# Softmax sums of the second attention layer: two query blocks per pass, straight from the statistics' tile, and the squares weighted once per batch

## The chip, the cores and the metric

The kernel runs on one core of one Trainium2 chip. A core has five engines that run side by side and meet through semaphores: TensorE (PE in the profile; its weight loads are shown apart as PEld), VectorE (DVE), ScalarE (ACT), GpSimd (POOL) and SyncE (SP), and 16 DMA engines that the queues of SP and POOL feed. The metric is the device time of one execution in microseconds (us). A figure given as a median is one of several executions; the profile shows one execution.

## The reference, cut to what matters

The input is 8 images of 512 channels by 1024 positions, all in float32. Two attention layers follow one another. Only the second is touched. With 8 heads of 64 channels it computes

```
attn = einsum('bhdq,bhdT->bhqT', q, k) * scale
attn = einsum('gh,bhqT->bgqT', w_head, attn)          # mixes the heads
attn = softmax(attn, axis=-1)
mean = mean(attn, axis=(-2, -1)); var = var(attn, axis=(-2, -1))
attn = (attn - mean) / sqrt(var + EPS) * in_gamma + in_beta
out  = einsum('bhqT,bhdT->bhqd', attn, v) ... @ w_proj.T + b_proj
```

So each row of the mixed scores needs its sum of exponentials Z (the softmax divides by it), and each head needs the sum over all rows of (sum of squared exponentials) / Z squared, from which the variance follows. The mean is known: a row of a softmax adds up to 1.

## The kernel before, in words

The first layer takes the first 1800 us or so. Then the eight images (batches) go through the second layer one after the other. The 1024 query rows of a batch are cut into 8 blocks of 128, called p = 0 to 7. A block is pipelined over three steps; step p does, in four parts t = 0 to 3, the scores of block p, the head mixing, the exponentials, the transposes and the statistics of block p-1, and the products with V of block p-2. `Attention1.step` writes that order out by hand, and it is the order on every engine: nothing moves past it.

What one block goes through:

- `scores` (L1628): PE makes q times k; ACT copies the result from PSUM to the tile `raw` (L1640).
- `regroup` (L1646): SP issues 16 DMAs of 256 KB per block that rearrange `raw` into the tile `re`, so that heads lie on partitions. `raw` has two buffers, so a copy of the next block waits until the DMAs have read the old contents.
- `mix` (L1665): PE mixes the heads; ACT takes the exponentials into `e` (L1678), two instructions for each of the four parts s of a block. The tile `e` has two buffers.
- `flip` (L1693): DVE transposes `e` into `et`. `moments` (L1704): DVE runs four `bn_stats` over the same `e`. Each leaves, for every partition, count, mean and sum of squared deviations of 256 even and of 256 odd elements; the access pattern is such that these are the two rows r of the part.
- `values` (L1720): PE multiplies V with `et` into an accumulator in PSUM; `leave` (L1736): ACT copies it into the output tile, in the place of q.
- `sums` (L1746 to L1750): three small DVE instructions turn mean and squared deviation into the sum (256 times the mean) and the sum of squares, in the tile `zz`.
- `totals` (L1757): PE adds these over the four partition groups with two matmuls against a 0/1 matrix `sel`; the results lie in PSUM. Below, this place in the order is called **stop p** (stop 0 to 7 of a batch). Stop p lies in part t = 1 of step p + 2, between products with V (L1720) and scores (L1628), which the mixing (L1665) follows.
- `reciprocals` (L1769 to L1789): DVE takes 1/Z, copies Z to `zs`, squares 1/Z, multiplies with the sum of squares and adds to a running sum `s2`: five small instructions, each block. 1/Z goes by one DMA to DRAM (`zd`, 4 KB, L1772) and by a second one back, broadcast over 64 partitions (`rzb`, 256 KB, L1779). POOL issues both, and for the last block SP.
- `divide` (L1811): after two blocks, when both halves of `rzb` are there, POOL multiplies the outputs of the pair by it (DVE for the last pair).
- At the end of a batch `instance` and `instance_end` make the variance from `s2`; `check` looks at the range of Z.

PSUM buffers for scores and mixing are three (`m_psum`), for products with V and the stops two (`acc_psum`). Tiles of the pool `stat` have two buffers if nothing else is said.

Of the kernel before, what the change touches and what calls it, by code (L numbers as in the profile page):

```python
# [18 lines left out]
P = 128  # L19
# [448 lines left out]
def tile_two_attention_layers(  # L468
# [33 lines left out]
    dram = ctx.enter_context(tc.tile_pool(name="dram", bufs=1, space=DRAM))  # L502
# [13 lines left out]
    def const_tile(name, shape, dt=F32):  # L516
        return const.tile(shape, dt, tag=name, name=name)
# [15 lines left out]
    ones = const_tile("ones", [P, P])  # L533
# [30 lines left out]

    sel = const_tile("sel", [P, 32])
    nc.vector.reduce_sum(sel, ident.rearrange("p (c j) -> p j c", c=4), axis=AX.X)
    init.close()


# [3 lines left out]
    chk = const_tile("chk", [P, 2, NCHK])  # L573
# [123 lines left out]
    with ExitStack() as l0:  # L697
# [4 lines left out]
        zpool = l0.enter_context(tc.tile_pool(name="zpool", bufs=2))  # L702
        stat = l0.enter_context(tc.tile_pool(name="stat", bufs=2))
# [563 lines left out]
    with ExitStack() as l1:  # L1267
# [5 lines left out]
        zpool = l1.enter_context(tc.tile_pool(name="zpool1", bufs=1))  # L1273
        stat = l1.enter_context(tc.tile_pool(name="stat1", bufs=2))
# [17 lines left out]
        NF = 5  # L1292
        re_t = repool.tile([P, NF + 4, 2, FB], F32, tag="re", name="re")
# [319 lines left out]
        class Attention1:  # L1613
            def __init__(self, b):
                self.b = b
                self.raw, self.e, self.et, self.acc, self.bn = {}, {}, {}, {}, {}
                self.pieces = []
                self.zs = stat.tile([32, NT, 32], F32, tag="zs", name=f"zs_{b}", bufs=1)
                self.s2 = stat.tile([32, 32], F32, tag="s2", name=f"s2_{b}")

            def scores(self, p, i):

# [74 lines left out]

            def moments(self, p, s):

                if s == 0:  # L1700
                    self.bn[p] = stat.tile([P, 4, 4, 6], F32, tag="bn1", name=f"bn1_{self.b}_{p}")
                e = self.e.pop((p, s))
                for a in range(4):
                    nc.vector.bn_stats(  # L1704
                        self.bn[p][:, s, a], e[:, :, a].rearrange("p r k -> p k r")
                    )

            def values(self, p, u, *parts):
# [29 lines left out]
                        acc[two * D : two * D + D].rearrange("p a (r x) -> p a r x", r=2),  # L1738
                    )

            def sums(self, p):

                bn = self.bn.pop(p).rearrange("p s a (r k) -> p r (s a) k", k=3)
                zz = stat.tile([P, 3, 2, 16], F32, tag="zz", name=f"zz_{self.b}_{p}")
                mean, m2 = bn[..., 1], bn[..., 2]
                nc.vector.tensor_scalar_mul(  # L1746
                    zz[:, 0::2], mean.unsqueeze(1).to_broadcast([P, 2, 2, 16]), float(2 * P)
                )
                nc.vector.tensor_mul(zz[:, 1], mean, zz[:, 0])
                nc.vector.tensor_add(zz[:, 1], zz[:, 1], m2)  # L1750
                self.zz = zz

            def totals(self, p):

                ps = acc_psum(f"z1_{self.b}_{p}")
                for m in range(2):
                    nc.tensor.matmul(  # L1757
                        ps[:D, ts(m, 32)],
                        self.zz[:, m : m + 2].rearrange("p m r c -> p (m r c)"), sel,
                        start=True, stop=True,  # L1760
                    )
                self.reciprocals(p, ps)

            def reciprocals(self, p, ps):

                b = self.b
                z, z2 = ps[:32, 0:32], ps[:32, 32:64]
                rz = stat.tile([32, 32], F32, tag="rz", name=f"rz1_{b}_{p}")
                nc.vector.reciprocal(rz, z)  # L1769
                zd = dram.tile([H, P], F32, tag=f"zd_{b}_{p}", name=f"zd_{b}_{p}")  # L1770
                queue = nc.sync if p == NT - 1 else nc.gpsimd
                queue.dma_start(  # L1772
                    out=zd.rearrange("g (x q) -> x g q", q=4),
                    in_=rz.rearrange("x (g q) -> x g q", q=4),
                )
                if p % 2 == 0:
                    self.rzb = zpool.tile([P, T], F32, tag="rzb", name=f"rzb_{b}_{p}")
                h = p % 2 * D
                queue.dma_start(  # L1779
                    out=self.rzb[h : h + D], in_=zd.rearrange("g i -> (g i)").partition_broadcast(D)  # L1780
                )
                nc.vector.tensor_copy(self.zs[:, p], z)
                r2 = stat.tile([32, 32], F32, tag="r2", name=f"r2_{b}_{p}")
                nc.vector.tensor_mul(r2, rz, rz)  # L1784
                if p == 0:
                    nc.vector.tensor_mul(self.s2, r2, z2)
                else:
                    nc.vector.tensor_mul(r2, r2, z2)
                    nc.vector.tensor_add(self.s2, self.s2, r2)  # L1789

            def check(self):

                b = self.b
                zs = self.zs.rearrange("p t c -> p (t c)")
                junk = zpool.tile([P, T], F32, tag="rzb", name=f"junk_{b}")[:32, : NT * 32]
                cnt = stat.tile([32, 2], F32, tag="cnt", name=f"cnt_{b}")
                nc.vector.tensor_scalar(
                    junk, zs, Z_MAX, 0.0, ALU.is_lt, ALU.add, accum_out=cnt[:, 0:1]
                )
                nc.vector.tensor_scalar(  # L1800
                    junk, zs, 1.0 / RZ_MAX, 0.0, ALU.is_gt, ALU.add, accum_out=cnt[:, 1:2]
                )
                nc.vector.tensor_add(cnt[:, 0:1], cnt[:, 0:1], cnt[:, 1:2])
                nc.vector.tensor_scalar(
                    chk[:32, 1, B * H + b : B * H + b + 1], cnt[:, 0:1],
                    -(2.0 ** 60), 2.0 ** 61 * NT * 32, ALU.mult, ALU.add,
                )

            def divide(self, n, engine=nc.vector):
# [3 lines left out]
            def instance(self):  # L1813

                b = self.b
                self.sb = stat.tile([32, H], F32, tag="isb", name=f"isb_{b}")
                nc.vector.reduce_sum(
                    self.sb, self.s2.rearrange("p (g q) -> p g q", q=4), axis=AX.X
                )

            def instance_end(self, ps=None):
                b = self.b
                if ps is None:
                    ps = small_psum1(f"pi_{b}")
                nc.tensor.matmul(ps[:, :H], ones[:32], self.sb, start=True, stop=True)
# [21 lines left out]
            def step(self, p, t, ag):  # L1847

                new, old, older = p < NT, p >= 1, p >= 2
                if t == 0:  # L1850
# [3 lines left out]
                    if older:  # L1854
                        self.values(p - 2, 0, 2, 3)
                        self.leave(p - 2, 0)
                        self.sums(p - 2)
                        if p % 2 == 0 and p >= 4:
                            self.divide(p // 2 - 2, nc.gpsimd)
                    if old:  # L1860
# [2 lines left out]
                elif t == 1:  # L1863
                    if older:
                        self.values(p - 2, 1, 0)
                        self.flip(p - 1, 0)
                        self.totals(p - 2)
                        self.moments(p - 1, 0)
                    if new:
                        self.scores(p, 3)  # L1870
# [51 lines left out]
        for b in range(B):  # L1922
            more = b + 1 < B
            a = Attention1(b)
# [37 lines left out]
            ag.flush()  # L1962
            k_leave()
            last = NT - 1
            a.sums(last)
            if not more:
                a.values(last, 0, 2, 3)
                a.leave(last, 0)
                a.values(last, 1, 0, 1, 2, 3)
                a.leave(last, 1)  # L1970
                a.totals(last)
                a.instance()
                out1_last(a)
                continue
# [3 lines left out]
            load_wv(b + 1)  # L1978
            a.values(last, 1, 0, 1, 2, 3)
            a.leave(last, 1)  # L1980
            a.totals(last)
            a.instance()
            k_leave()
            k_go(4, 3)
# [84 lines left out]
```

## Time and profile before

| | us |
|---|---|
| runs | 3997.65, 3999.17, 4006.88 (median 3999.17) |
| profiled execution, its own time | 3999.31 |
| span of the profile (first to last instruction) | 3997.5 |
| PE busy (share of the span) | 3885.5 (97%) |
| DVE busy | 2834.6 (71%) |
| ACT busy | 1971.3 (49%) |
| POOL busy | 128.5 (3%) |
| granted TensorE clock, mean | 0.995 |

How to read it: the shares are means over very different stages. In the second layer a batch takes about 277 us; of these some 170 us are the nine steps of the attention, the rest are the projections, where PE works alone. Inside the steps DVE is nearly as full as PE (18 to 25 us of DVE work in a step of 21 to 26 us), so which of the two makes the other wait has to be read from the waits and the timeline, place by place.

### The profile page before, as it was taken

The numbers are of one execution on the slowest core, as the hardware profiler recorded it, in microseconds if no ns is written. First come the engines' busy times: TensorE is split into PE (matmuls) and PEld (weight loads), VectorE is DVE, ScalarE is ACT, GpSimd is POOL, SyncE is SP. The second block draws the span as 40 slices with busy tenths as digits, with TensorE's granted clock in tenths as the row PEclk, the third lists the DMA queues.
The fourth block names the chain that finished last, engine by engine and source line by source line (L and its number), as shares of the span: only waits on it lengthen the run. The fifth ranks groups of instructions, "written<-read, shape, count | busy, mean of one in ns | idle before, by whom it ended". The sixth has DMA issues, their size and how long they took to land.

```text
span 3997.5 us, 95841 instructions
## 1 busy us (share of the span) xinstructions
PE 3885.5 (97%) x41932; PEld 1826.1 (46%) x41932; DVE 2834.6 (71%) x4124; ACT 1971.3 (49%) x2431; POOL 128.5 (3%) x150
## 2 busy tenths in 40 slices
PE   8999999999999999999999999999999999999997
PEld 4353535344343535344544535545545445445354
DVE  4748475766657584857958949859769679588597
ACT  1726363544536271615717528437257166175274
POOL 0000000000000000000100000000001000000010
PEclk9999999999999999999999999999999999999999
DMA  3313131111121111217828749658469288397384
GB/s 121 120 48 117 46 120 48 62 59 66 53 83 54 72 68 61 75 66 184 230 92 226 190 120 237 173 137 227 148 164 228 99 210 207 97 232 198 107 219 127
DMA packets 245883, 519.10 MB, mean 130 GB/s; under 512 B 47312, under 2 KB 54480, under 8 KB 238800
## 3 DMA queue, kind: packets, MB, share of 16 engines
q1 hardware_dynamic: 238912, 497.95, 43.2%
q0 software_dynamic: 6544, 14.94, 1.7%
q8 instruction: 331, 5.42, 0.6%
q14 instruction: 96, 0.79, 0.1%
HBM read 197.16 MB, written 46.92 MB: 61 GB/s over the span
## 4 chain that ended last, share of the span: by engine, by line
PE 81%; DVE 13%; ACT 2%; DMA 2%; issue 2%; SPq 0%; DVEq 0%
PE s L1084 11%; PE a L1110 11%; PE a L1720 7%; PE s L1628 7%; DVE bn L1704 6%; PE pk_p L902 6%; PE pq_p L902 5%; PE pv L1454 5%; PE pv_p L902 5%; DVE et L1693 5%; PE pp_p L902 5%; PE pk L1379 4%; PE pq L1379 4%; PE pp L1379 4%; PE m L1665 4%
## 5 line engine op out<-in xcount | busy, mean ns | idle before, releaser
L1693 DVE STREAM_TRANSPOSE et<-e 128x2048 f32<-128x2048 f32 x256 | 587.3, 2294 | 88.7 <-ACT e L1678 86.8
L1720 PEld LDWEIGHTS a<-et,v 128*64 128x64 f32 x16384 | 509.2, 138 | 296.2 <-issue 247.6
L1704 DVE BATCH_NORM_STATS2 bn<-e 128x6 f32<-128x512 f32 x1024 | 634.3, 675 | 0.0
L1089 ACT ACTIVATE e<-s 128x1024 f32<-128x1024 f32 x512 | 497.2, 1026 | 234.5 <-PE s L1084 232.1
L1640 ACT COPY raw<-s 128x1024 f32<-128x1024 f32 x480 | 470.2, 1018 | 226.1 <-PE s L1628 197.5
L1720 PE MATMUL a<-et,v 128*64 128x64 f32 x16384 | 557.0, 225 | 12.1 <-DVE et L1693 11.4
L1678 ACT ACTIVATE e<-m 128x1024 f32<-128x1024 f32 x512 | 496.2, 1021 | 126.5 <-PE m L1665 54.2
L1097 DVE TENSOR_TENSOR zacc<-zacc,e 128x1024 f32<-128x1024 f32 x384 | 468.7, 1221 | 87.2 <-ACT e L1089 64.9
L1628 PE MATMUL s<-k,q 64*64 64x512 f32 x4096 | 516.0, 608 | 6.2 <-DVE q L1493 3.1
L1084 PE MATMUL s<-q,k 64*64 64x512 f32 x4096 | 490.1, 593 | 2.3 <-ACT e L1089 2.3
L1110 PE MATMUL a<-e,v 64*64 64x512 f32 x4096 | 484.1, 589 | 0.0
L1665 PE MATMUL m<-re,wmix 32*32 32x512 f32 x8192 | 315.3, 604 | 19.3 <-DMA re<-raw 17.8
L1110 PEld LDWEIGHTS a<-e,v 64*64 64x64 f32 x4096 | 156.7, 133 | 282.8 <-issue 282.2
L1084 PEld LDWEIGHTS s<-q,k 64*64 64x64 f32 x4096 | 147.9, 133 | 275.2 <-issue 240.7
L1628 PEld LDWEIGHTS s<-k,q 64*64 64x64 f32 x4096 | 127.7, 132 | 220.8 <-issue 78.2
L1454 PE MATMUL pv<-wv,y 128*128 128x512 f32 x480 | 212.1, 597 | 0.0
L1736 ACT COPY q<-a 64x256 f32<-64x256 f32 x256 | 93.7, 366 | 184.7 <-PE a L1720 182.7
L1772 POOL DMA_DIRECT2D zd<-rz x56 | 34.7, 619 | 3449.0 <-DVE r L1784 3449.0
L1454 PEld LDWEIGHTS pv<-wv,y 128*128 128x128 f32 x480 | 89.3, 190 | 116.9 <-issue 110.3
L1665 PEld LDWEIGHTS m<-re,wmix 32*32 32x32 f32 x8192 | 66.7, 103 | 148.9 <-ACT raw L1640 58.6
L1458 ACT COPY v<-pv 128x512 f32<-128x512 f32 x30 | 17.6, 585 | 218.7 <-PE pv L1454 218.7
L1095 DVE TENSOR_TENSOR zacc<-e,e 128x1024 f32<-128x1024 f32 x64 | 78.3, 1223 | 56.1 <-ACT e L1089 56.1
(315 smaller groups left out, 3942.4 us busy)
## 6 DMA issues: line engine op xcount, KB each, us to landing
re<-raw SPq DMA_DIRECT2D x1024, 256.0 KB
left_q<-left_q SPq DMA_DIRECT2D x17, 1792.0 KB
left_p<-left_p SPq DMA_DIRECT2D x17, 1792.0 KB
left_k<-left_k SPq DMA_DIRECT2D x10, 1792.0 KB
x<-in_x_dram SPq DMA_DIRECT2D x32, 512.0 KB
rzb<-zd SPq DMA_DIRECT2D x128, 128.0 KB
x<-x SPq DMA_DIRECT2D x64, 256.0 KB
y<-x SPq DMA_DIRECT2D x32, 512.0 KB
```

Of the source, the lines that this page charges most:

```text
L902: nc.tensor.matmul(out, st, mv, start=start, stop=(k == 1), skip_group_check=True)
L1084: nc.tensor.matmul(ps[c * D : c * D + D, m], k[r, hp, k0 : k0 + D], q[r, hp, ts(f, FB)], start=True, stop=True,)
L1089: nc.scalar.activation(e[i], ps, AF.Exp, scale=S0 * S0)
L1110: nc.tensor.matmul(acc[g][a][m * D : m * D + D], v[rows, kc, ts(2 * hp + m, D)], e[i][rows, m], start=(kc == 0), stop=(kc == NG - 1),)
L1379: nc.tensor.matmul(self.ps[m][:, i], w[:, left, k * HC + i * P : k * HC + i * P + P], right[:, k], start=(k == 0 and m != 2), stop=(k == 1 ...
L1454: nc.tensor.matmul(ps[:, m], y_t[b][:, c, ts(2 * i + m, P)], w[:, c], start=(c == 0), stop=(c == NCC - 1),)
L1628: nc.tensor.matmul(ps[c * D : c * D + D, m], qo_t[b][r, p, hp, ts(c, D)], k_t[b][r, hp, ts(kh, FB)], start=True, stop=True,)
L1665: nc.tensor.matmul(ps[a // 2][c * 32 : c * 32 + 32, a % 2].rearrange("p (r h k) -> p h r k", r=2, h=2), wmix[rows].rearrange("p g i -> p ( ...
L1678: nc.scalar.activation(e[:, :, 2 * h : 2 * h + 2].rearrange("p r a k -> p a r k"), ps[h].rearrange("p a (r k) -> p a r k", r=2), AF.Exp,)
L1693: nc.vector.transpose(self.et[p, u].rearrange("p kb (r st a) g q -> p st kb r (a g q)", r=2, st=2)[:, st], self.e[p, s].rearrange("p r a ( ...
L1704: nc.vector.bn_stats(self.bn[p][:, s, a], e[:, :, a].rearrange("p r k -> p k r"))
L1720: nc.tensor.matmul(acc[two * D : two * D + D, s].rearrange("p (x q) -> p x q", q=4), v_t[b][:, kb, ts(g, D)], et[:, kb, :, g], start=(kb = ...
```

## The change

`moments` collects the statistics of two blocks, 2n and 2n+1, in one tile. `sums` and `totals` then run once per pair, in the step in which the odd block had them; the even block's stop no longer exists. At the stop that is left three matmuls read the statistics' tile itself: the means against `sel256` (the 0/1 matrix times 256, made once at the start), the squared deviations against `sel`, and the squared means (times 256) against `sel`, added in PSUM. Only the squared means need a DVE instruction (`sq`). DVE then takes 1/Z of 64 rows and copies sum and sum of squares to `zs`. What weighted the squares block by block goes to `instance`, once per batch over all four pairs: reciprocal, square, product and reduction over 128 elements per partition, in a free slot of `re`.

The rows of a pair lie on 64 partitions as (block t, column c, row r), so 1/Z leaves in four DMAs of 2 KB (for r, for t) in place of two of 4 KB, and comes back in two of 256 KB, one right behind the other, where they were one per step. For the last pair SP issues all six.

```diff
+    sel256 = const_tile("sel256", [P, 32])
+    nc.vector.tensor_scalar_mul(sel256, sel, float(2 * P))
...
-                self.zs = stat.tile([32, NT, 32], F32, tag="zs", name=f"zs_{b}", bufs=1)
-                self.s2 = stat.tile([32, 32], F32, tag="s2", name=f"s2_{b}")
+                self.zs = stat.tile([64, NCH, 64], F32, tag="zs", name=f"zs_{b}", bufs=1)
...
+                n = p // 2
+                if s == 0 and p % 2 == 0:
+                    self.bn[n] = stat.tile(
+                        [P, 2, 4, 4, 6], F32, tag="bn1", name=f"bn1_{self.b}_{n}"
+                    )
...
-                zz = stat.tile([P, 3, 2, 16], F32, tag="zz", name=f"zz_{self.b}_{p}")
-                mean, m2 = bn[..., 1], bn[..., 2]
-                nc.vector.tensor_scalar_mul(
-                    zz[:, 0::2], mean.unsqueeze(1).to_broadcast([P, 2, 2, 16]), float(2 * P)
-                )
-                nc.vector.tensor_mul(zz[:, 1], mean, zz[:, 0])
-                nc.vector.tensor_add(zz[:, 1], zz[:, 1], m2)
...
+            def sums(self, n):
+                mean = self.stats(n)[:, :, 1]
+                self.sq = stat.tile([P, 64], F32, tag="sq", name=f"sq_{self.b}_{n}", bufs=1)
+                nc.vector.scalar_tensor_tensor(
+                    self.sq, mean, float(2 * P), mean, ALU.mult, ALU.mult
+                )
...
+            def totals(self, n):
+                b, last = self.b, n == NCH - 1
+                bn = self.stats(n)
+                ps = acc_psum(f"z1_{b}_{n}")
+                nc.tensor.matmul(ps[:64, :32], bn[:, :, 1], sel256, start=True, stop=True)
+                for i, x in enumerate((bn[:, :, 2], self.sq)):
+                    nc.tensor.matmul(ps[:64, 32:64], x, sel, start=(i == 0), stop=(i == 1))
+                rz = stat.tile([64, 32], F32, tag="rz", name=f"rz1_{b}_{n}")
+                nc.vector.reciprocal(rz, ps[:64, :32])
+                nc.vector.tensor_copy(self.zs[:, n], ps[:64, :64])
+                zd = dram.tile([2, H, P], F32, tag=f"zd_{b}_{n}", name=f"zd_{b}_{n}")
+                queue = nc.sync if last else nc.gpsimd
+                for r in range(2):
+                    for t in range(2):
+                        queue.dma_start(
+                            out=zd[t].rearrange("g (r c q) -> r c g q", r=2, q=4)[r],
+                            in_=rz[32 * t + r : 32 * t + 32 : 2].rearrange("c (g q) -> c g q", q=4),
+                        )
+                self.rzb = zpool.tile([P, T], F32, tag="rzb", name=f"rzb_{b}_{n}")
+                for t in range(2):
+                    queue.dma_start(
+                        out=self.rzb[t * D : t * D + D],
+                        in_=zd[t].rearrange("g i -> (g i)").partition_broadcast(D),
+                    )
...
-                r2 = stat.tile([32, 32], F32, tag="r2", name=f"r2_{b}_{p}")
-                nc.vector.tensor_mul(r2, rz, rz)
-                if p == 0:
-                    nc.vector.tensor_mul(self.s2, r2, z2)
-                else:
-                    nc.vector.tensor_mul(r2, r2, z2)
-                    nc.vector.tensor_add(self.s2, self.s2, r2)
...
             def instance(self):
+                scr = re_t[:64, NF + 3, 0]
+                z, z2 = self.zs[:, :, :32], self.zs[:, :, 32:]
...
+                nc.vector.reciprocal(r, z)
+                nc.vector.tensor_mul(r, r, r)
+                nc.vector.tensor_mul(
+                    s2, r.rearrange("p n (g q) -> p n g q", q=4),
+                    z2.rearrange("p n (g q) -> p n g q", q=4),
+                )
                 nc.vector.reduce_sum(
...
-                        self.sums(p - 2)
+                        if p % 2:
+                            self.sums(p // 2 - 1)
...
-                        self.totals(p - 2)
+                        if p % 2:
+                            self.totals(p // 2 - 1)
```

More of the change, by code (lines that the diff above doesn't have):

```diff
@@ L1698, in moments @@
             def moments(self, p, s):
-                if s == 0:
-                    self.bn[p] = stat.tile([P, 4, 4, 6], F32, tag="bn1", name=f"bn1_{self.b}_{p}")
+                n = p // 2
[3 more added lines that the diff above has]
+                    )
                 e = self.e.pop((p, s))
@@ L1704, in moments @@
                     nc.vector.bn_stats(
-                        self.bn[p][:, s, a], e[:, :, a].rearrange("p r k -> p k r")
+                        self.bn[n][:, p % 2, s, a], e[:, :, a].rearrange("p r k -> p k r")
                     )
@@ L1739, in leave @@
                     )
-            def sums(self, p):
-                bn = self.bn.pop(p).rearrange("p s a (r k) -> p r (s a) k", k=3)
-                zz = stat.tile([P, 3, 2, 16], F32, tag="zz", name=f"zz_{self.b}_{p}")
-                mean, m2 = bn[..., 1], bn[..., 2]
-                nc.vector.tensor_scalar_mul(
-                    zz[:, 0::2], mean.unsqueeze(1).to_broadcast([P, 2, 2, 16]), float(2 * P)
-                )
-                nc.vector.tensor_mul(zz[:, 1], mean, zz[:, 0])
-                nc.vector.tensor_add(zz[:, 1], zz[:, 1], m2)
-                self.zz = zz
@@ L1753, in totals @@
[L1753 to L1760, printed above, removed]
-                    )
[L1762 to L1774, printed above, removed]
-                )
[L1776 to L1782, printed above, removed]
-                r2 = stat.tile([32, 32], F32, tag="r2", name=f"r2_{b}_{p}")
-                nc.vector.tensor_mul(r2, rz, rz)
-                if p == 0:
-                    nc.vector.tensor_mul(self.s2, r2, z2)
-                else:
-                    nc.vector.tensor_mul(r2, r2, z2)
-                    nc.vector.tensor_add(self.s2, self.s2, r2)
@@ new lines, in stats @@
+            def stats(self, n):
+                return self.bn[n].rearrange("p t s a (r k) -> p (t s a r) k", k=3)
+            def sums(self, n):
[3 more added lines that the diff above has]
+                    self.sq, mean, float(2 * P), mean, ALU.mult, ALU.mult
+                )
+            def totals(self, n):
+                b, last = self.b, n == NCH - 1
+                bn = self.stats(n)
+                del self.bn[n]
+                ps = acc_psum(f"z1_{b}_{n}")
[18 more added lines that the diff above has]
+                        in_=zd[t].rearrange("g i -> (g i)").partition_broadcast(D),
+                    )
@@ L1791, in check @@
             def check(self):
                 b = self.b
-                zs = self.zs.rearrange("p t c -> p (t c)")
-                junk = zpool.tile([P, T], F32, tag="rzb", name=f"junk_{b}")[:32, : NT * 32]
-                cnt = stat.tile([32, 2], F32, tag="cnt", name=f"cnt_{b}")
+                zs = self.zs[:, :, :32]
+                junk = zpool.tile([P, T], F32, tag="rzb", name=f"junk_{b}")[
+                    :64, : NCH * 32
+                ].rearrange("p (n c) -> p n c", n=NCH)
+                cnt = stat.tile([64, 2], F32, tag="cnt", name=f"cnt_{b}")
@@ L1804, in check @@
                 nc.vector.tensor_scalar(
-                    chk[:32, 1, B * H + b : B * H + b + 1], cnt[:, 0:1],
-                    -(2.0 ** 60), 2.0 ** 61 * NT * 32, ALU.mult, ALU.add,
+                    chk[:64, 1, B * H + b : B * H + b + 1], cnt[:, 0:1],
+                    -(2.0 ** 60), 2.0 ** 61 * NCH * 32, ALU.mult, ALU.add,
                 )
@@ L1815, in instance @@
                 b = self.b
-                self.sb = stat.tile([32, H], F32, tag="isb", name=f"isb_{b}")
+                self.sb = stat.tile([64, H], F32, tag="isb", name=f"isb_{b}")
+                scr = re_t[:64, NF + 3, 0]
+                z, z2 = self.zs[:, :, :32], self.zs[:, :, 32:]
+                r = scr[:, : NCH * 32].rearrange("p (n c) -> p n c", n=NCH)
+                s2 = scr[:, NCH * 32 : 2 * NCH * 32].rearrange("p (g n q) -> p n g q", n=NCH, q=4)
+                nc.vector.reciprocal(r, z)
[4 more added lines that the diff above has]
+                )
                 nc.vector.reduce_sum(
-                    self.sb, self.s2.rearrange("p (g q) -> p g q", q=4), axis=AX.X
+                    self.sb,
+                    scr[:, NCH * 32 : 2 * NCH * 32].rearrange("p (g x) -> p g x", g=H), axis=AX.X,
                 )
@@ L1824, in instance_end @@
                     ps = small_psum1(f"pi_{b}")
-                nc.tensor.matmul(ps[:, :H], ones[:32], self.sb, start=True, stop=True)
+                nc.tensor.matmul(ps[:, :H], ones[:64], self.sb, start=True, stop=True)
                 var = stat.tile([P, H], F32, tag="ivar", name=f"ivar_{b}")
@@ L1964, in tile_two_attention_layers @@
             last = NT - 1
-            a.sums(last)
+            a.sums(NCH - 1)
             if not more:
@@ L1970, in tile_two_attention_layers @@
                 a.leave(last, 1)
-                a.totals(last)
+                a.totals(NCH - 1)
                 a.instance()
@@ L1980, in tile_two_attention_layers @@
             a.leave(last, 1)
-            a.totals(last)
+            a.totals(NCH - 1)
             a.instance()
```

## The prediction

> **What bounds the kernel now.** First the page's busy shares and chain, then who waits on PE, then the timeline around the stops, then the DMA queues.
>
> ```profile
> PE 3885.5 (97%) x41932; PEld 1826.1 (46%) x41932; DVE 2834.6 (71%) x4124; ACT 1971.3 (49%) x2431; POOL 128.5 (3%) x150
> PE 81%; DVE 13%; ACT 2%; DMA 2%; issue 2%; SPq 0%; DVEq 0%
> L1757 PE MATMUL z<-sel,zz 128*64 128x32 f32 x256 | 24.9, 220 | 32.8 <-DVE zz L1750 29.1 <-ACT e L1678 3.6
> ...
> PE z L1757 <- DVE zz L1750: 29.1, 27, 2.1
> PE m L1665 <- DMA re<-raw: 17.8, 11, 3.3
> PE z L1757 <- ACT e L1678: 3.6, 18, 0.4
> PE m L1665 <- ACT e L1678: 1.4, 8, 0.2
> ```
>
> PE is the bound. It idles 112 us in the whole span (3997.5 - 3885.5), and the largest single wait is the one at the stops: 32.8 us before L1757, nearly all of it for `zz`. So DVE time counts only where it ends a wait of PE. The small DVE instructions that go are some 104 us busy (64 blocks by 1.62 us, the means of L1746 to L1789 added up); the new ones come to some 35 us. Were DVE the bound, that would be 68 us; it is not.
>
> Stop 0 and stop 4 of the second batch:
>
> ```profile
> 2131.58 1.94 ACT L1678 ACTIVATE e<-m 128x1024 f32<-128x1024 f32 x2 [0.48 <-ACT q L1736]
> 2133.32 0.21 DVE L1750 TENSOR_TENSOR zz<-zz,bn 128x32 f32<-128x32 f32 x1
> 2133.68 0.39 PE L1757 MATMUL z<-sel,zz 128*64 128x32 f32 x4 [1.22 <-DVE zz L1750]
> 2134.00 1.09 PE L1628 MATMUL s<-k,q 64*64 64x512 f32 x8
> 2135.02 1.16 PE L1665 MATMUL m<-re,wmix 32*32 32x512 f32 x32
> ...
> 2217.13 1.94 ACT L1678 ACTIVATE e<-m 128x1024 f32<-128x1024 f32 x2 [0.64 <-ACT q L1736]
> 2219.70 0.39 PE L1757 MATMUL z<-sel,zz 128*64 128x32 f32 x4 [1.66 <-DVE zz L1750]
> 2220.01 1.09 PE L1628 MATMUL s<-k,q 64*64 64x512 f32 x8
> 2221.03 1.16 PE L1665 MATMUL m<-re,wmix 32*32 32x512 f32 x32
> ```
>
> In brackets stands PE's idle time. A stop itself takes 0.31 us of PE (2219.70 to 2220.01). Over eight batches the idle time before stops 0 to 7 adds up to 9.8, 1.5, 3.4, 1.9, 13.0, 1.4, 1.8 and 0 us. The even stops, which go, hold 28.0 of the 32.8.
>
> **The change, part by part.** *Even stops: what comes next.* Without a stop PE goes on with the scores (1.02 us) and then the mixing, which needs the second exponential's PSUM buffer back (the row "m waits for e": 1.4 us in 8 places). At stop 0 PE would be ready at 2133.68 - 1.22, done with the scores at 2133.48, but the exponentials end at 2131.58 + 1.94 = 2133.52; with 0.06 for the signal the mixing starts at 2133.58 instead of 2135.02: 1.44 us, in each of 8 batches alike, 11.5 us. At stop 4 the same sum gives 2219.13 instead of 2221.03, the idle time plus 0.24: 13.0 + 8 x 0.24 = 14.9 us. At stop 2 (idle about 0.5 us) the exponentials allow 0.72 us in six batches, 0.60 in one and nothing in one: 4.9 us. Stop 6 has no idle time in seven batches; its 0.31 us each make 2.2 us. In the last batch DVE leads after stop 6 (PE later waits 5.33 us for a transpose): the three `zz` that delay a transpose from about 3930.15 to 3930.67 and the 0.87 us of the five small instructions behind it go: 1.4 us. Sum 34.9 us.
>
> *Does DVE follow?* After stop 4 of the second batch PE is 1.9 us earlier. The second transpose (L1693, 2224.99 to 2227.2) moves up by the 0.5 us or more that DVE saved before and the 0.6 us of small instructions behind the first one, to an end near 2226.05; the products that need it move from 2229.20 to 2227.2. It holds, with 1 us spare.
>
> *Odd stops.* Three matmuls in place of two: 0.31 x 6/4 = 0.47 us, 0.16 more, 32 times: 5.1 us lost. The first needs only `bn`, the third `sq`, one instruction (about 0.23 us, as L1746) for three. The 0.2 us of idle time at stops 1, 3 and 5 remains: there ACT's first exponential, not DVE, releases the stop (the row with 18 waits). About 0.9 us of the 4.8 goes. Net 4.2 us lost.
>
> *Strided weights.* The stops load `bn` with 12 bytes between elements. No weight load in the trace is strided. The nearest row, the moving operand of L1720 in runs of 16 bytes, takes 225 ns against 220 for L1757's dense one: I take nothing. Upper bound, a second load's time (138 ns) for each of 4 x 32 strided loads: 17.7 us; a gain is excluded, the old loads being dense. [...]
>
> *The two broadcasts at once.* This is the part to fear.
>
> ```profile
> DMA packets 291, 0.55 MB, mean 276 GB/s; under 512 B 31, under 2 KB 31, under 8 KB 290
> q1 hardware_dynamic: 288, 0.53, 94.1%
> ...
> DMA packets 190, 0.46 MB, mean 228 GB/s; under 512 B 26, under 2 KB 26, under 8 KB 190
> q0 software_dynamic: 69, 0.24, 55.3%
> q1 hardware_dynamic: 121, 0.22, 44.7%
> ...
> 2171.25 2.84 ACT L1640 COPY raw<-s 128x1024 f32<-128x1024 f32 x3 [1.72 <-DMA re<-raw]
> ```
>
> These are the DMA queues in the 2 us before `rzb` moves (2205 to 2207) and while it does (2207 to 2209), and a copy of ACT behind another `rzb`. q1 carries the regrouping, 4 MB per step, and loses 0.31 MB, 1.1 us of its pace. The waits show where that ends: ACT's copies to `raw` wait 22.9 us in 21 places for regrouping DMAs, 1.72 us in the line shown. Today one `rzb` comes per step; now two follow in the steps of stops 1, 3 and 5, none in the others. POOL issues four `zd` (0.61 us each) instead of one, then both `rzb`: the first starts about 1.1 us later than today's, the second 0.6 us behind it. So regrouping there ends some 1.1 us later; bounds 0 (it only moves from one step to the next, and DMAs have idle moments) and 2.5 us (the longest such wait of ACT is 2.33). Three places feel it. Before stop 2's place ACT's copies have 0 to 1.2 us to spare, by batch; what exceeds that adds up to 4.2 of the 4.9 us. Before stop 4's place the copies wait behind a normalization anyway: 0.3 us a batch, 2.4 us. In step 8 the first mixing already waits for its DMAs (1.2 to 3.3 us, 16.7 us in all); `rzb` will end about when these DMAs begin (2253.44 in the second batch): 0.4 us a batch, 3.2 us. Together 9.8 us. Relief in the other steps hides behind stop 3 and 5's ACT wait.
>
> [...]
>
> *End of a batch.* DVE gets reciprocal, two products, a reduction over 128 elements: 0.77 (from 312 ns for 32 and 196 ns for 8 elements) + 2 x 0.31 + 0.26 = 1.65 us, so its queue behind stop 7, L1400 first, slips about 1.0 us. Cover: PE multiplies until 2300.4, and the last L1435 waits 2.21 us for it; without cover 8 us. SP issues three `zd` (0.33) and one `rzb` (0.49) more: the loads behind it slip 1.5 us and have 1.8 us until SP waits for PE anyway (2300.54). `divide` on DVE starts 13 us after the `rzb` issue, in the last batch 5.9 us; there it may slip 2 to 3 us, and the products that need it are 7 us off. Nothing taken. `sel256` adds 0.1 us to the start.
>
> *Sum:* 34.9 - 4.2 - 9.8 - 0.1 = 20.8 us. Against the profiled execution's 3999.31 (span 3997.5 plus 1.8 around it; the median of the runs is 3999.17) that is 3978.5, say 3978.
>
> **Rivals.** *The bursts hide (0.24).* DMAs that catch up within the step cost nothing: 34.9 - 4.2 gives 30.7 less, 3968. For it: DMAs fall idle for a microsecond or two right after most stops. Against: the 1.72 us wait of ACT shown above follows an `rzb`.
>
> *A burst costs more (slower, 0.10).* The three places per batch make 24 of them; each further microsecond there costs up to 24 us. From 1.1 + 20.8/24 = 2 us on the change loses; at 2.5 us the time is 3978 + 1.4 x 24 = 4012. For it: DMA share 0.94 in the steps with other loads. Against: the second 256 KB is no more than the first, which costs 1.1.
>
> *The wait only moves (0.14).* Bursts of 1.5 to 2 us, or half the bound of the strided loads on top, leave 0 to 11 us: about 3993, the same within 0.3%.
>
> **How the numbers follow.** Forecast 0.52, own range 3970 to 3987. 0.3% is 12 us, about what a measurement of this kernel tells from no change. Faster by more: 0.52 + 0.24 = 0.76; same 0.14; slower 0.10. The range takes in the hidden bursts, 5 us of slack below, and most of the third rival: 3963 to 3993.
>
> **What would show it.** In the profile after: L1757's successors 192 matmuls, with under 8 us of idle time; a new row "m waits for e" of some microseconds; "m waits for DMA re" above 17.8 by about 3; "raw waits for DMA re" above 22.9, in half as many places; DVE busy lower by 60 to 70 us; weight loads at the stops still near 138 ns. I am wrong if the idle time reappears before L1720 (transposes late after all), or if step 8's wait grows by more than 1 us a batch.

## The result, and the profile after

The changed kernel takes as long as the one before: medians of 4001.4 us after and 4001.9 us before on the same chip, a ratio of 0.9995 with a 95% interval of 0.9988 to 1.0003. The prediction was 3978 us. The profiled execution of the changed kernel took 3994.71 us, with a span of 3992.9.

First the busy shares on the page of the changed kernel. Line numbers move by one to nine: mixing is L1666, the exponentials L1679, the transposes L1694, the products with V L1724, the stop L1762 and L1764.

```profile
PE 3888.9 (97%) x41868; PEld 1827.5 (46%) x41868; DVE 2772.4 (69%) x3741; ACT 1974.3 (49%) x2431; POOL 141.1 (4%) x182
```

Then, in the same kernel, who waits on PE and on ACT (in total, times, longest, in us):

```profile
PE m L1666 <- DMA re<-raw: 40.3, 22, 4.8
...
PE m L1666 <- ACT e L1679: 1.4, 8, 0.2
...
ACT raw L1641 <- DMA re<-raw: 9.5, 6, 3.2
```

The wait for `zz` (32.8 us with ACT's part) is gone, no row of the stops is left, and DVE has 62 us less to do. In its place the mixing waits 40.3 us for regrouping DMAs, where it waited 17.8.

Stop 4's former place in the second batch, in the timeline (start, length, then in brackets PE's idle time ahead):

```profile
2214.26 1.15 PE L1666 MATMUL m<-re,wmix 32*32 32x512 f32 x32 [1.00 <-DMA re<-raw]
...
2215.34 1.15 PE L1724 MATMUL a<-et,v 128*64 128x64 f32 x32
...
2216.43 1.09 PE L1629 MATMUL s<-k,q 64*64 64x512 f32 x8
...
2217.44 1.28 PE L1666 MATMUL m<-re,wmix 32*32 32x512 f32 x32
```

Products, scores and mixing now follow each other without a gap; the 1.66 us of idle time and the stop are gone. But the mixing that opens the step waited 1.00 us for DMAs, and in the kernel before that mixing waited 0.10.

The largest waits are in step 8. PE's timeline of the changed kernel, second batch:

```profile
2251.81 1.10 PE L1724 MATMUL a<-et,v 128*64 128x64 f32 x32
2257.39 1.98 PE L1666 MATMUL m<-re,wmix 32*32 32x512 f32 x32 [4.48 <-DMA re<-raw]
2259.30 4.53 PE L1381 MATMUL pk<-y,left_k 128*128 128x512 f32 x8
2263.76 1.15 PE L1724 MATMUL a<-et,v 128*64 128x64 f32 x32
```

and the same place in the kernel before:

```profile
2258.78 1.15 PE L1665 MATMUL m<-re,wmix 32*32 32x512 f32 x32 [2.40 <-DMA re<-raw]
2259.87 3.70 PE L1379 MATMUL pk<-y,left_k 128*128 128x512 f32 x8
2263.50 1.15 PE L1720 MATMUL a<-et,v 128*64 128x64 f32 x32
```

Two things are worse. The wait is 4.48 us in place of 2.40. And the same 32 matmuls behind it last 1.98 us in place of 1.15, the next 8 last 4.53 in place of 3.70. The windows of the changed kernel say why (window, width, then busy time and instructions of PE, its weight loads, DVE, ACT and POOL; then the granted clock, the DMA share and GB/s):

```profile
2256.00:2257.00 1.00, 0.00 (x0) 0.00 (x0) 1.00 (x3) 0.00 (x0) 1.00 (x1) 1.00 1.08 262
2257.00:2258.00 1.00, 0.61 (x16) 0.28 (x32) 1.00 (x2) 0.00 (x0) 0.97 (x1) 0.79 1.07 260
2258.00:2259.00 1.00, 1.00 (x32) 0.00 (x0) 1.00 (x1) 0.00 (x0) 0.00 (x0) 0.50 1.06 256
2259.00:2260.00 1.00, 1.00 (x17) 0.50 (x2) 0.97 (x2) 0.56 (x1) 0.00 (x0) 0.50 1.07 260
2260.00:2261.00 1.00, 1.00 (x2) 0.34 (x1) 0.32 (x1) 1.00 (x2) 0.00 (x0) 0.50 1.08 258
2261.00:2262.00 1.00, 1.00 (x4) 0.43 (x3) 0.59 (x1) 0.38 (x1) 0.00 (x0) 1.00 1.07 270
```

As the wait ended TensorE was granted half its clock, here from 2257.59 to 2261.00 by the clock records of the trace. Apart from the one in which the span ends, such a stretch ("half clock" below) lasted 3.41 us, or twice that, in the records, and cost about half its length: here 1.98 - 1.15 and 4.53 - 3.70, 1.7 us together. In the changed kernel one begins at the end of each of the eight waits of step 8, from 1.2 us before it to 0.9 us after; in the kernel before, at two of the eight.

Where did the DMAs lose the time? The DMA queues of the changed kernel, from 2246 to 2248, then in the three stretches of 2 us that follow:

```profile
q1 hardware_dynamic: 271, 0.49, 88.5%
...
q1 hardware_dynamic: 132, 0.24, 58.1%
q0 software_dynamic: 53, 0.20, 35.5%
...
q0 software_dynamic: 78, 0.25, 54.2%
q1 hardware_dynamic: 118, 0.22, 51.4%
...
q1 hardware_dynamic: 154, 0.29, 82.3%
q0 software_dynamic: 26, 0.07, 18.4%
```

q0 carries the two broadcasts, q1 the regrouping (packets, MB, share of the 16 engines). So in 6 us it is short of 3 x 0.49 - (0.24 + 0.22 + 0.29) = 0.72 MB, which is 2.9 us at its own pace. These 6 us lie where the second half of block 7's regrouping runs, and the mixing that waits 4.48 us needs it.

The balance by steps follows from the starts of the first mixing of each block: row p is the time from block p-1's to block p's, added up over eight batches, so it holds stop p-2 where there is one. The columns e1 to e8 are the runs told of below. Each column is one execution, the profiled one; that of the changed kernel is 6.7 us faster than its median and that of e6 7.3 us, so a difference of a microsecond or two between columns means little. The last row adds row 7 of the eight batches (stop 5) and the times from block 7's first mixing to block 0's of the next batch, of which there are seven; in parentheses stands what the half clock cost in it, the length of its stretches times one half (a little too much where a stretch begins while PE still waits).

| us | before | after | e1 | e2 | e3 | e4 | e5 | e6 | e7 | e8 |
|---|---|---|---|---|---|---|---|---|---|---|
| row 2 (stop 0) | 175.9 | 165.3 | 165.1 | 165.0 | 165.0 | 175.7 | 175.6 | 165.1 | 164.9 | 165.4 |
| row 3 (stop 1) | 168.0 | 172.7 | 166.5 | 166.9 | 167.3 | 174.9 | 167.4 | 172.1 | 167.1 | 167.2 |
| row 4 (stop 2) | 170.8 | 166.1 | 164.2 | 165.7 | 169.2 | 172.8 | 171.1 | 164.8 | 165.3 | 165.9 |
| row 5 (stop 3) | 168.0 | 173.0 | 166.9 | 166.4 | 167.7 | 179.0 | 167.4 | 170.5 | 166.9 | 168.2 |
| row 6 (stop 4) | 184.8 | 166.8 | 164.4 | 167.8 | 172.0 | 174.1 | 175.5 | 166.5 | 166.4 | 168.1 |
| row 7 and on to the next batch | 1067.1 (3.4) | 1089.2 (15.5) | 1066.0 (3.4) | 1073.0 (8.7) | 1066.1 (3.4) | 1096.4 (19.8) | 1068.4 (5.1) | 1058.9 (0) | 1067.6 (5.1) | 1055.0 (0) |

(Row 6 of the kernel before holds 5.1 us of half clock that the other columns don't.) The rows of the even stops are 10.6, 4.7 and 18.0 us shorter: the gain is there. Rows 3 and 5 are 4.7 and 5.0 us longer, the last row 22.1, of which 12.1 are half clock. Gain and loss cancel.

### The profile page after: what moved, and what is told of

It reads as the page before. It is cut to its first block, busy times and chain, and to the rows that moved or that the text cites. A ratio compares the mean times of both kernels' runs of the same rounds, so it can differ in the third digit from the quotient of the medians.

```text
span 3992.9 us, 95453 instructions
## 1 busy us (share of the span) xinstructions
PE 3888.9 (97%) x41868; PEld 1827.5 (46%) x41868; DVE 2772.4 (69%) x3741; ACT 1974.3 (49%) x2431; POOL 141.1 (4%) x182
## 5 line engine op out<-in xcount | busy, mean ns | idle before, releaser
L1694 DVE STREAM_TRANSPOSE et<-e 128x2048 f32<-128x2048 f32 x256 | 589.8, 2304 | 155.8 <-ACT e L1679 148.6
L1724 PEld LDWEIGHTS a<-et,v 128*64 128x64 f32 x16384 | 508.0, 138 | 296.2 <-issue 273.2
L1679 ACT ACTIVATE e<-m 128x1024 f32<-128x1024 f32 x512 | 496.9, 1023 | 149.7 <-PE m L1666 51.4
L1724 PE MATMUL a<-et,v 128*64 128x64 f32 x16384 | 555.8, 224 | 13.1 <-DVE et L1694 10.4
L1666 PE MATMUL m<-re,wmix 32*32 32x512 f32 x8192 | 324.0, 610 | 43.8 <-DMA re<-raw 40.3
L1772 POOL DMA_DIRECT2D zd<-rz x96 | 52.5, 552 | 3537.2 <-DVE rz L1766 3535.1
L1666 PEld LDWEIGHTS m<-re,wmix 32*32 32x32 f32 x8192 | 70.8, 103 | 174.2 <-ACT raw L1641 68.6
```

What stands on the lines that cost most here:

```text
L1666: nc.tensor.matmul(ps[a // 2][c * 32 : c * 32 + 32, a % 2].rearrange("p (r h k) -> p h r k", r=2, h=2), wmix[rows].rearrange("p g i -> p ( ...
L1679: nc.scalar.activation(e[:, :, 2 * h : 2 * h + 2].rearrange("p r a k -> p a r k"), ps[h].rearrange("p a (r k) -> p a r k", r=2), AF.Exp,)
L1694: nc.vector.transpose(self.et[p, u].rearrange("p kb (r st a) g q -> p st kb r (a g q)", r=2, st=2)[:, st], self.e[p, s].rearrange("p r a ( ...
L1724: nc.tensor.matmul(acc[two * D : two * D + D, s].rearrange("p (x q) -> p x q", q=4), v_t[b][:, kb, ts(g, D)], et[:, kb, :, g], start=(kb = ...
```

## The experiments

Two theories stood against each other. *Burst:* two broadcasts in one step hold back that step's regrouping. *Transfers as a second bound:* regrouping, 4 MB per step, takes back whatever PE saves, broadcasts or not.

**e1: the changed kernel without the broadcasts of pairs 0 to 2.**

```diff
                 self.rzb = zpool.tile([P, T], F32, tag="rzb", name=f"rzb_{b}_{n}")
+                if not last:
+                    nc.gpsimd.memset(self.rzb, 1.0)
+                    return
                 for t in range(2):
```

> The changed kernel without the broadcasts of pairs 0 to 2: POOL fills the tile `rzb` with ones instead (so the outputs of these pairs are not divided by Z); the small DMAs `zd` stay. Two theories. Burst: the two broadcasts that follow each other in the steps of stops 1, 3 and 5 hold back the second half of that step's regrouping, and the mixing of blocks 3, 5 and 7 waits for it (40.3 us of PE's idle time in the changed kernel, 30.1 of them at block 7 and the rest at blocks 2 to 5). Then this kernel loses all of the waits at blocks 3 and 5 and at least half of those at block 7: mixing waits for DMAs below 20 us, time 20 to 35 us below the kernel before, some 3965 to 3980. Transfers as a second bound: regrouping alone (4 MB per step at about 250 GB/s, 16 of 20.5 us) takes back what PE saves, with the broadcasts or without. Then the waits stay above 30 us and the time within 10 us of the kernel before.

Measured: 3952.1 us, a ratio of 0.9884 (0.987 to 0.9899), 47 us less than the kernel before. PE's waits and ACT's:

```profile
PE m L1666 <- DMA re<-raw: 18.6, 11, 3.3
...
ACT raw L1641 <- DMA re<-raw: 1.1, 3, 0.4
```

More than the burst theory had said, and far from the other: PE runs ahead of the changed kernel here, and yet the mixing waits half as long. At blocks 3 and 5 only 0.2 us of its waits are left; at block 7 there are still 17.8 us, without any broadcast, as many as in the kernel before (16.7). That wait is what regrouping by itself cannot hide, and little more.

**e2: one broadcast per step.** The second broadcast waits, on POOL, for the exponentials of the next step's first mixing.

```diff
-                for t in range(2):
+                self.zd = zd
+                self.back(queue, range(2) if last else range(1))
...
-                        if p % 2 == 0 and p >= 4:
-                            self.divide(p // 2 - 2, nc.gpsimd)
+                        if p % 2 and p >= 5:
+                            self.divide((p - 1) // 2 - 2, nc.gpsimd)
                     if old:
                         self.mix(p - 1, 0)
+                    if p % 2 == 0 and p >= 4:
+                        mark = stat.tile([1, 1], F32, tag="mark", name=f"mark_{self.b}_{p}")
+                        nc.gpsimd.tensor_copy(mark, self.e[p - 1, 0][:1, 0, 3, 255:])
+                        self.back(nc.gpsimd, range(1, 2))
+                        if p == NT:
+                            self.divide(p // 2 - 2, nc.gpsimd)
```

(`back` issues the broadcasts of the halves named, with the lines that stood in `totals`.)

> The changed kernel with the second of the two broadcasts held back to the next, even step (behind that step's first mixing, by a one-element copy on POOL that waits for its exponentials), so that each step has one as in the kernel before; the division of the pair follows one step later. Burst: the waits at blocks 3 and 5 go, those at block 7 fall from 30.1 to about the 16.7 us of the kernel before; mixing waits for DMAs about 18 us, time about 20 us below the kernel before (3975 to 3985). Transfers as a second bound: the same bytes, so the same sum of waits (35 to 45 us), part of them now at blocks 2, 4 and 6; time within 6 us of the kernel before.

Measured: 3968.4 us, ratio 0.9923 (0.9911 to 0.9935), 31 us less than the kernel before and somewhat better than even the burst theory had said. POOL's timeline in the second batch shows the edit at work:

```profile
2194.08 2.18 POOL L1772 DMA_DIRECT2D zd<-rz  x4 [14.22 <-DVE rz L1766]
2199.84 0.54 POOL L1783 DMA_DIRECT2D rzb<-zd  x1 [3.58 <-DMA zd<-rz]
2212.07 0.17 POOL L1875 COPY mark<-e 1x1 f32<-1x1 f32 x1 [11.70 <-ACT e L1679]
2212.58 0.52 POOL L1783 DMA_DIRECT2D rzb<-zd  x1 [0.33 <-issue]
```

and PE's waits its effect:

```profile
PE m L1666 <- DMA re<-raw: 21.4, 12, 3.2
```

The same bytes, the same stops, the same DVE work, one broadcast moved by a step: some 30 us against the changed kernel. (The pair's division moves by a step with it; it is not the cause, since it stands in its old place both in e1, which gains more, and in e4, which loses as much.) The theory of transfers as a second bound, which had the same waits in other places, falls. Rows 3 and 5 give back 5.8 and 6.6 us, the last row 16.2 (6.8 of them half clock).

**e3: both broadcasts one step later.** As e2, with nothing issued at the stop and both behind the next step's first mixing (shown against e2).

```diff
-                self.back(queue, range(2) if last else range(1))
+                self.back(queue, range(2) if last else range(0))
...
-                        self.back(nc.gpsimd, range(1, 2))
+                        self.back(nc.gpsimd, range(0, 2))
```

> The changed kernel with both broadcasts held back to the next, even step, behind its first mixing, when the regrouping that the mixing waits for is done and the next one has a whole step before it is needed. If a burst of two hurts wherever it is: waits of about 40 us, now at blocks 4 and 6 (block 7 free, as there is no regrouping in step 8), time about 3990 to 4000. If it hurts only by its place ahead of the second half of a step's regrouping: waits below 15 us, block 7 below the 16.7 us of the kernel before, time 3965 to 3975. Transfers as a second bound: waits 35 to 45 us in all, time within 6 us of the kernel before.

Measured: 3970.1 us, ratio 0.9929 (0.9916 to 0.9942), 29 us less. Who waits on PE and ACT:

```profile
PE m L1666 <- DMA re<-raw: 21.4, 17, 3.4
...
ACT raw L1641 <- DMA re<-raw: 19.6, 9, 3.4
```

The time is the one expected if the place decides, but the waits are not (below 15 us were expected, and 17.7 stand at block 7 alone), and the rows tell otherwise. Rows 3 to 6 add up to 662.0 us without broadcasts (e1), 666.8 with one per step (e2), 676.2 here and 678.6 in the changed kernel: with regrouping under way a burst costs 14 to 17 us in these rows in either step, and apart its halves cost 5. In the even steps, where the burst now falls, the delay shows more at ACT's copies (19.6 us) than at the mixing, the route that the prediction had named. The gain over the changed kernel is in the last row: pair 2's burst in step 8, without regrouping, costs nothing (1066.1, and 1066.0 without broadcasts).

**e4: only the burst.** The kernel before, with the even block's `zd` and broadcast held to the odd stop.

```diff
-                queue.dma_start(
-                    out=zd.rearrange("g (x q) -> x g q", q=4),
-                    in_=rz.rearrange("x (g q) -> x g q", q=4),
-                )
...
+                self.half.append((p, zd, rz))
+                if p % 2 or p == NT - 2:
+                    for _, d, r in self.half:
+                        queue.dma_start(
+                            out=d.rearrange("g (x q) -> x g q", q=4),
+                            in_=r.rearrange("x (g q) -> x g q", q=4),
+                        )
+                    for i, d, _ in self.half:
+                        h = i % 2 * D
+                        queue.dma_start(
+                            out=self.rzb[h : h + D],
+                            in_=d.rearrange("g i -> (g i)").partition_broadcast(D),
+                        )
+                    self.half = []
```

> The kernel before, with all its stops and its small instructions, but the even block's `zd` and broadcast held back to the odd stop, so that two broadcasts follow each other there; the last pair as before. Only the burst of the change, with none of its savings. Burst: mixing waits for DMAs rise from 17.8 to 27 us or more, most of it at block 7, and the kernel is 5 to 15 us slower than the one before. Transfers as a second bound: the bytes and PE's pace are those of the kernel before, so waits (17.8) and time stay, within 3 us.

Measured: 4035.1 us, a ratio of 1.0084 (1.0067 to 1.01): 36 us more, over twice what even the burst theory had said. PE's waits:

```profile
PE m L1665 <- DMA re<-raw: 35.9, 19, 4.1
PE z L1757 <- DVE zz L1750: 21.0, 23, 1.5
```

and PE's timeline in step 8 of the second batch:

```profile
2266.41 2.02 PE L1665 MATMUL m<-re,wmix 32*32 32x512 f32 x32 [4.11 <-DMA re<-raw]
2268.36 5.75 PE L1379 MATMUL pk<-y,left_k 128*128 128x512 f32 x8
2274.04 1.15 PE L1720 MATMUL a<-et,v 128*64 128x64 f32 x32
```

The mixing's 18 us of added wait are half of it. In step 8 the work that took 4.72 us in the kernel before (2258.78 to 2263.50) now takes 7.63 (2266.41 to 2274.04), with half the clock from 2265.70 to 2272.53, and in the last row of the table the half clock costs 16.4 us more than in the kernel before; that part the expectation had left out. Here `zd` goes out in two DMAs, as before, not in four: the price is that of the broadcasts.

**e5: the kernel before without the broadcasts of blocks 0 to 5.**

```diff
-                queue.dma_start(
-                    out=self.rzb[h : h + D], in_=zd.rearrange("g i -> (g i)").partition_broadcast(D)
-                )
+                if p < NT - 2:
+                    nc.gpsimd.memset(self.rzb[h : h + D], 1.0)
+                else:
+                    queue.dma_start(
+                        out=self.rzb[h : h + D],
+                        in_=zd.rearrange("g i -> (g i)").partition_broadcast(D),
+                    )
```

> The kernel before without the broadcasts of blocks 0 to 5: POOL fills those parts of the tile `rzb` with ones (so the outputs of these blocks are not divided by Z); all stops and small instructions stay. Against the changed kernel without broadcasts (47 us below the kernel before) it gives what the change's own saving is where no broadcast disturbs. If the stops are worth what the prediction gave them (34.9 - 4.2 = 30.7 us), this kernel is 13 to 20 us below the kernel before, since the single broadcasts then cost it some 16 us. If the stops were worth less and the 47 us are mostly the price of broadcasts, single ones included, it is 30 us or more below it. If single broadcasts cost the kernel before nothing, it stands within 5 us of it.

Measured: 3983.5 us, ratio 0.9951 (0.9934 to 0.9967): 18 us less. That is within the 13 to 20 us expected if the stops are worth what the prediction gave them. So the change by itself, where no broadcast disturbs, is worth 47 - 18 = 29 us (some 20 to 38 by the two intervals), and single broadcasts cost the kernel before some 18 us (13 to 26).

**e6: work ahead of the wait.** The changed kernel, with the first 8 matmuls of the next projection ahead of block 7's first mixing.

```diff
+                    if not new:
+                        ag.run(4 * p - 0.5)
                     if old:
                         self.mix(p - 1, 0)
```

> The changed kernel with one thing moved: in step 8 the first 8 matmuls of the next batch's projection (`pk`, 3.7 us, which stood right behind the first mixing) go ahead of that mixing (in the last batch there is nothing to move). The broadcasts stay as they are. PE idles 30.1 us ahead of block 7's mixing, and in the records the granted clock falls to half for windows of 3.41 us, one or two of them right after each of the eight waits. If that half clock follows from PE's idle time, filling it takes both away: the waits of seven batches (25 us) and 11 to 16 us of lost clock; 30 to 40 us below the kernel before, 3960 to 3970. If the clock falls for another reason, only the waits go: 20 to 25 us below. If the rest of step 8 was waiting for transposes anyway, the wait moves there and the time stays within 8 us of the kernel before.

Measured: 3965.5 us, ratio 0.9912 (0.9896 to 0.9929), 36 us less than the kernel before. PE's timeline in step 8 of the second batch:

```profile
2246.91 3.70 PE L1381 MATMUL pk<-y,left_k 128*128 128x512 f32 x8
2250.55 1.14 PE L1666 MATMUL m<-re,wmix 32*32 32x512 f32 x32
2251.62 1.15 PE L1724 MATMUL a<-et,v 128*64 128x64 f32 x32
2252.97 2.05 PE L1666 MATMUL m<-re,wmix 32*32 32x512 f32 x32 [0.20 <-ACT e L1679]
```

The time is the one expected if the half clock follows from PE's idle time. In seven batches the wait is filled (in three of them 0.3 to 1.3 us of it are left), and no half clock is left there, though nothing else was done about the clock: in step 8 it follows from PE's idle time. The last line shows what the move costs: the second mixing now comes right after the products and waits for the exponentials of the first (2.05 us in place of 1.14, and 0.20 of idle time).

**e7 and e8: the two together.** e7 is e2 for pairs 0 and 1 and e3 for pair 2 (shown against e2); e8 adds the move of e6.

```diff
-                self.back(queue, range(2) if last else range(1))
+                self.back(queue, range((1, 1, 0, 2)[n]))
...
-                        self.back(nc.gpsimd, range(1, 2))
+                        self.back(nc.gpsimd, range(1 if p < NT else 0, 2))
```

> The changed kernel with the second broadcast of pairs 0 and 1 held back by one step, and both of pair 2 held back into step 8, which has no regrouping. By the sums per step of the two runs before, the first is best for steps 3 to 6 and the second for steps 7 and 8: 35 to 40 us below the kernel before, some 5 us below the run with one broadcast per step. If step 8's loads are delayed by the two broadcasts there, it is no better than that run (31 us below).

> The run before this one and the projection's first 8 matmuls ahead of the mixing of block 7 together: if the two add up, waits of mixing for DMAs below 8 us, next to no half clock between the steps and the next batch, and 55 to 65 us below the kernel before (3935 to 3945). If the moved matmuls delay the exponentials of step 8 and so the transposes, 40 us below or less.

Measured: e7 3960.4 us, ratio 0.9897 (0.988 to 0.9914); e8 3951.8 us, ratio 0.9873 (0.9857 to 0.989). The first is 41 us below the kernel before, a little better than expected. The second is the fastest kernel that leaves nothing out, 50 us below the kernel before (e1, without broadcasts, took 3952.1 us), though the two don't add up: in the last row e8 gains 12.6 us on e7, though 15.1 us of waits for DMAs at block 7 and 5.1 us of half clock went. The second mixing's wait for exponentials, as in e6's last line, takes the rest back: 0.20 us of idle time and 0.9 us of its length in each of seven batches, 7.8 us. Two of PE's waits in e8:

```profile
PE a L1724 <- DVE et L1694: 10.4, 9, 5.3
PE m L1666 <- DMA re<-raw: 4.4, 7, 2.2
```

## Why the prediction was wrong

*The even stops (34.9 us) came nearly as predicted.* Rows 2, 4 and 6 of the changed kernel are 33.3 us shorter, or 28.2 without the 5.1 us of half clock in the kernel before; without broadcasts (e5 to e1) they are 28.5 us shorter, where stops 0, 2 and 4 had been given 31.3. The 3.6 us of stop 6 can't be told apart from the end of the batch in these rows. DVE does follow: PE's wait for transposes went from 11.4 to 10.4 us. The whole saving by itself, 34.9 - 4.2 = 30.7 us, measured 29 (e1 against e5) and 31 (e2, with one broadcast per step as in the kernel before).

*The odd stops* were taken a little too dear. A stop of three matmuls holds PE for 0.53 us, not 0.47; but from e5 to e1 rows 3 and 5 became 1.4 us shorter, not longer, the wait for ACT being gone too.

*The strided weights* cost little, but not nothing. In the changed kernel, groups by operation with busy time and mean ns:

```profile
L1764 PEld LDWEIGHTS z<-sel,bn 128*64 128x64 f32 x64 | 8.4, 175 | 0.0
L1762 PEld LDWEIGHTS z<-sel,bn 128*64 128x64 f32 x64 | 8.1, 170 | 0.0
L1764 PEld LDWEIGHTS z<-sel,sq 128*64 128x64 f32 x64 | 6.5, 140 | 0.0
```

A quarter longer than the dense load of `sq`, 4.2 us of load time in 128 loads (which overlaps with matmuls in part: in the window 2259 to 2260 above PE is busy for 1.00 us and its loads for 0.50), nearer to the row taken (nothing) than to the upper bound (17.7). A second load's time for each, the upper bound, would have made 276 ns; the strided loads took 170 and 175.

*The two broadcasts (9.8 us): this step failed.* Measured, splitting them gives back some 30 us, and doubling them up in the kernel before costs 36. Its price for a burst was nearly right; where it put the delay, what it deducted and what it left out were wrong.

The route and its slack: the step let regrouping end 1.1 us later and looked for the effect at ACT's copies to `raw`, ahead of the places of stops 2 and 4, where it deducted slack. In the changed kernel these copies wait less than before, 9.5 us in place of 22.9. (5.1 of the 22.9 are a single wait at 1832.58, at the start of the layer, which e5 has without broadcasts too; the prediction's "longest, 2.33" is the longest of the others.) The delay ends at the mixing that opens the next step and needs the second half of that very regrouping, and there was too little slack to hide it: rows 3 and 5 are 5.8 and 6.6 us longer than with the broadcasts apart (e2), row 7 by 10.5 (174.2 and 163.7), 23 us or 0.95 us for each of 24 bursts. PE's earlier arrival is not what took the slack away: at the pace of the kernel before (e4) the same rows grow by more, 6.9, 11.0 and 17.0 us, 31.7 without the half clock in row 7 (3.2) and 1.3 for each burst. The 1.1 us per burst was a fair price; taken 24 times without slack it is 26 us, and the sum would have been 34.9 - 4.2 - 26 - 0.1 = 4.6 us, within the interval measured (4.8 us less to 1.2 us more).

The relief: it was put down to nothing because stops 3 and 5 wait for ACT. The even steps, without a broadcast now, gave nothing back, as it had said: row 4 of the changed kernel is 0.4 us longer than in e2, row 6 is 1.0 us shorter.

Step 8: given 0.4 us a batch, since the broadcasts were to end about as its DMAs begin. By the queues they ran from 2248 to 2254, and the regrouping that the mixing waits for ran beside them. The wait grew by 13.4 us in all (16.7 to 30.1), 1.7 us a batch; the prediction had named more than 1 us as what would prove it wrong. On top came 12.1 us of half clock, which it had not priced at all, though the trace of before has two such stretches behind waits of step 8. In the clock records of the changed kernel these stretches are 3.413 us long, or twice that, and their starts fit a grid of that length: those behind step 8's waits begin at 2257.59, 2534.07 and 2810.55, 276.48 apart, which is 81 times 3.413, and then at 3090.44, 279.89 later, 82 times. The length of the wait does not decide by itself: one of 1.41 us brought the half clock in the kernel before, and one of 3.38 us in e3 did not.

*The other signs.* The idle time at the stops is nil, the end of the batch costs nothing that shows (`instance` takes 945 + 283 + 282 + 278 ns = 1.79 us, given as 1.65; without half clock e1 and e5 take 901.0 and 900.9 us from block 7's first mixing to the next batch), DVE is 62 us less busy: right. "m waits for e" stayed at 1.4 us and did not grow.

*The rivals.* The forecast, 3978, and the hidden bursts, 3968, both put the bursts too cheap; 3968 is what e2 takes, where the broadcasts don't meet. "The wait only moves" (0.14, about 3993) came nearest, a burst that eats the gain, but it reached that by bursts of 1.5 to 2 us, where 0.95 us without slack and the half clock did it. "A burst costs more" (0.10), which needed 2 us or more for each, did not come about.

*Open:* why a broadcast of 0.25 MB takes more than that from q1 (0.36 MB for each of the two here), and which condition, beside the length of a wait, brings the half clock. Of the first the record shows this much: in the 6 us from 2248 to 2254 q0 moved 0.52 MB, and all queues together 1.28 MB where the 2 us ahead of them, at 0.51 MB, would have made 1.53; so the engines also moved less in all while the two queues ran side by side. Neither question was tried in a run.

## What to carry to other kernels

When two transfers that came one per step are put into one step, ask first which consumer needs the bytes that queue behind them, and when; here the wait showed at that consumer, not at the engine that waited on the queue before. Price the delay in full at each place, unless a trace shows slack at that consumer; slack at another engine doesn't count. And where a wait of PE cannot be removed, put work that needs nothing ahead of it: in step 8 of the changed kernel waits of 3.2 to 4.8 us cost themselves and then half of the 3.41 or 6.83 us of half clock that came with them.

## What the hardware showed

- Idle time of PE cost twice here. In the changed kernel, at the end of waits of 3.2 to 4.8 us, the granted clock was 0.50 for 3.41 or 6.83 us, in eight batches of eight; at waits of 1.2 to 3.4 us (before, e1, e3, e5) in some and not in others, so the length of the wait alone doesn't decide. In the seven batches where the wait was filled (e6, e8) it did not occur there at all.
- DVE time that was freed off the critical path stayed idle: in the changed kernel, which takes as long as the one before, DVE's wait for exponentials ahead of its transposes rose from 86.8 to 148.6 us, by the 62 us saved (in e1, 47 us faster, to 110.4).
- Weight loads of 64 float32 columns with 12 bytes between elements took 170 to 175 ns in the changed kernel, dense ones 140 there (`sq`) and 138 in the kernel before (`zz`).
